# Conv stage of a mixture-of-experts block: the layer norm in two phases, with more convolution steps between a block's phases

## The chip, the cores and the metric

The kernel runs on one core of one Trainium2 chip. The core has five engines, each with its own instruction queue that is worked through in order: TensorE (PE, matrix multiply, with its weight loads shown as PEld), VectorE (DVE), ScalarE (ACT), GpSimd (POOL) and SyncE (SP), and 16 DMA engines that move data between HBM and the on-chip memory. The metric is the time on the device in microseconds (us), the median of three runs. The profile is of another execution, in which the profiler was running; that one took 6457.23 us, and its trace spans 6455.5 us.

## The reference, cut to what matters

Two layers follow each other. Layer 0 takes `x` of shape (32, 128, 56, 56) and does

```python
x = depthwise_conv7x7(input, dw_kernel) + dw_bias           # per channel
x = (x - mean_c(x)) / sqrt(var_c(x) + 1e-6) * ln_gamma + ln_beta   # over the 128 channels of a pixel
logits = x @ Wg + bg                                         # 8 experts, best 2 of each pixel
# mixture of experts with a capacity, in an order of priority
out = input + x + layer_scale * moe(x, logits)
```

Layer 1 is a 3x3 dilated convolution, a batch norm, a Gelu, an attention and a gate in Fourier space, and a residual. The change touches layer 0 alone, and there only the part up to `logits`: the depthwise convolution, the norm over channels, the multiplication by `ln_gamma`, the addition of `ln_beta`, and the product with `Wg`. Everything is in float32.

## The kernel before, in words

The kernel has three stages: the conv stage (this change), a search of each expert's threshold with the experts' matrix products, and layer 1.

**Groups and steps.** The 32 images are taken in 8 groups of 4. A group's convolution is made in `NS = 16` steps of 8 channels (`conv`, L121 to L149). A step loads two tiles, `xt` (784 KB of pixels) and `wt` (448 KB of a banded form of the taps), through SyncE's DMA queue into pools with 3 buffers each. TensorE then makes two PSUM banks `psa` of it (L136), and VectorE evicts each bank into the group's tile `y` with the bias added (L144). `y` holds 128 pixels on its partitions, 98 columns and 128 channels; it has 2 buffers. A buffer of `xt` comes free, and so the load for three steps later can start, when the matmuls of its step are done.

**Blocks and phases.** When all 16 steps of a group are done, every pixel has its 128 channels, and the norm can be made. The group's 98 columns are cut into 7 blocks (`sizes`): six of 16 columns and one of 2. `block` returns the phases of one block as closures:

- `stats`: VectorE takes `bn_stats` of each column (L161), some small operations (L165 to L171), a square root on ScalarE (L172), and a reciprocal and the bias `nb` (L173, L174);
- `norm`: ScalarE normalises each column in place, sixteen activations per block (L181); VectorE then multiplies by `gB` and adds `bB`, over the whole block (L185), and ScalarE's queue issues the store of the block to HBM (`xf<-y`, L188). ScalarE's queue stands still until VectorE is done with the block;
- `across`: TensorE transposes the block into four PSUM banks `pyt` (L196), ScalarE copies them out as `yT` (L198);
- `logits`: TensorE multiplies by `Wg` (L206), ScalarE copies the result `lq` (L215);
- `back`: TensorE transposes it again (L220), VectorE adds `bg` (L223).

After the last block, `choose` finds the two best experts of each pixel on VectorE (L263 to L302, some 17 operations of up to 1.5 us) and stores three numbers per pixel as `meta` in 64-byte rows (`xf<-meta`, L299).

**What sets the order.** `plan` makes a table from convolution step to phases: phase number `i` of block `b` stands at step `b*3//2 + i`. While group g+1 is convolved, each step is followed by the phases of group g that stand at it, and `choose` comes one step after the last phase. With five phases the last one stands at step 13 and `choose` at 14. After the last group there are no convolution steps left, and the phases follow each other (the tail of the stage). From this program a scheduler makes each engine's order when the kernel is built; it stays close to the order written, but moves single instructions ahead where it expects room. So where `across` of a block stands in TensorE's order is fixed: TensorE waits there until the block is normalised, and every convolution step behind it waits with it. As built, TensorE's order in a group is: steps 0, 1, 2, transposes of block 0, step 3, transposes of block 1, and so on, the transposes of the last block after step 11, and then steps 12 to 15 with nothing but the last logits between them.

Of the kernel before, what the change touches and what calls it, by code (L numbers as in the profile page):

```python
# [71 lines left out]
def conv_seq_kernel(ctx: ExitStack, tc: tile.TileContext, t: dict, out: bass.AP, dbg: dict):  # L72
# [41 lines left out]
    with tc.tile_pool(name="a1", bufs=1) as a1, tc.tile_pool(name="a2", bufs=2) as a2, tc.tile_pool(  # L114
# [9 lines left out]
        def conv(g, c0, y):  # L124

            xt = a3.tile([PK, CB, 4 * NCB * NB], F32, name="xt")
            nc.sync.dma_start(out=xt, in_=t["x8"][g, c0 // CB])
            wt = a3.tile([PK, CB, 2, P8 * P8], F32, name="wt")
            nc.sync.dma_start(out=wt, in_=t["wt"][c0 // CB])
            xv = xt.rearrange("k c (h n q) -> k c h n q", h=2, n=2)  # L130
            for c4 in range(0, CB, 4):
                ps = bank("psa")
                for c in range(4):
                    for b in range(2):
                        for h in range(2):
                            nc.tensor.matmul(  # L136
                                ps[h * 64 : (h + 1) * 64, c * TG : (c + 1) * TG],
                                lhsT=wt[:, c4 + c, b, :],
                                rhs=xv[:, c4 + c, h, :, b * NB : b * NB + NP],
                                start=(b == 0),  # L140
                                stop=(b == 1),
                            )
                cs = slice(c0 + c4, c0 + c4 + 4)
                nc.vector.tensor_tensor(  # L144
                    out=y[:, :, cs],
                    in0=ps[:, : 4 * TG].rearrange("p (c t) -> p t c", c=4),
                    in1=dwbB[:, cs].unsqueeze(1).broadcast_to([128, TG, 4]),
                    op=ALU.add,
                )  # L149

        def block(g, y, lg, t0, n):
# [26 lines left out]
            def norm():  # L178
                for i in range(n):
                    yi = y[:, t0 + i, :]  # L180
                    nc.scalar.activation(  # L181
                        yi, yi, AF.Identity, scale=sd[:, i : i + 1], bias=nb[:, i : i + 1]
                    )
                for w, op in ((gB, ALU.mult), (bB, ALU.add)):
                    nc.vector.tensor_tensor(  # L185
                        out=yb, in0=yb, in1=w.unsqueeze(1).broadcast_to([128, n, C]), op=op
                    )
                nc.scalar.dma_start(out=xfv[:, g * TG + t0 : g * TG + t0 + n, :C], in_=yb)  # L188
# [40 lines left out]
            else:  # L229
# [12 lines left out]
                def back():  # L242
# [4 lines left out]
                        op=ALU.add,  # L247
                    )

            return [stats, norm, across, logits, back]  # L250

        def choose(g, lg):

# [55 lines left out]


        NS = C // CB
        sizes = [16] * (TG // 16) + ([TG % 16] if TG % 16 else [])

        def plan(g, y):
            lg = a2.tile([128, TG, E], F32, name="lg")
            at = {}
            t0 = 0
            for b, n in enumerate(sizes):
                for i, phase in enumerate(block(g, y, lg, t0, n)):
                    at.setdefault(b * 3 // 2 + i, []).append(phase)  # L320
                t0 += n
            last = max(at)
            at[last + 1] = [lambda: choose(g, lg)]
            return at

        behind = {}
        for g in range(HI // 2):
            y = a2.tile([128, TG, C], F32, name="y")
            for k in range(NS):
                conv(g, k * CB, y)  # L330
                for phase in behind.pop(k, []):
                    phase()
            for k in sorted(behind):
                for phase in behind[k]:
                    phase()
            behind = plan(g, y)
# [970 lines left out]
```

## Time and profile before

| | |
|---|---|
| Time, median of 3 runs | 5591.87 us (5589.1 to 5595.34) |
| Span of the profiled execution | 6455.5 us, 85506 instructions |
| Busy: PE, PEld, DVE, ACT, POOL | 76%, 52%, 48%, 32%, 41% of the span |
| Conv stage in the trace | from the start to about 1068 us, then the store of the last `meta` to 1083.5 us |
| In the conv stage: `conv` matmuls L136 | 424.2 us busy |
| `norm` on ScalarE, L181 | 311.0 us busy, 784 activations, 488 ns each |
| `gB` and `bB` on VectorE, L185 | 48 of each for full blocks, 2284 and 2272 ns |
| transposes L196, idle time of PE ahead of them | 154.7 us busy, 304.4 us idle |

How to read it: a row of a group of instructions has the line, the engine, the operation, its operands by name and how many there were, then the busy time of the group, the mean duration of one, and behind a second bar the idle time of that engine just ahead of these instructions, with what ended it. A row of a window has the busy time of every engine in that stretch of the trace, the clock that TensorE was granted, the busy share of the DMA engines (it can go above 1 where packets overlap) and what they moved. Starts and ends of single instructions are read from the timeline.

### The profile page before, as it was taken

To read this page: it belongs to the slowest core of one execution; us is meant where nothing else is said; L and a number is where in the kernel's file an instruction comes from. 1 tells how busy PE (TensorE), PEld (TensorE's weight loads), DVE (VectorE), ACT (ScalarE), POOL (GpSimd) and SP (SyncE) were. 2 spreads that over 40 slices of the span, in tenths; PEclk is the share of its full clock that TensorE was granted. 3 is DMA by queue.
4 is the path that set the end of the run, shared out by engine and by line. 5 is a ranking of instruction groups with operands and counts; after the bars stand their busy time and mean duration, and the time that the engine had idled before them with its cause. 6 is when DMAs were issued, how large, how long until landed. Compare 5 with 4: busy or idle time off the path is not lost.

```text
span 6455.5 us, 85506 instructions
## 1 busy us (share of the span) xinstructions
PE 4925.6 (76%) x32850; PEld 3344.5 (52%) x32850; DVE 3087.3 (48%) x6927; ACT 2090.8 (32%) x3595; POOL 2616.6 (41%) x2564
## 2 busy tenths in 40 slices
PE   6666653598887989999984677777776876777678
PEld 5555552376665756766762344434444443444445
DVE  4676675565656655345221334434443443444346
ACT  2445543132232323333330223333332333333235
POOL 0000000344353435444436645565555545555450
PEclk8888885799999999999996778888887887888789
DMA  9999983122222222222233233333333333333331
GB/s 229 220 233 214 227 201 83 36 65 62 52 67 51 70 54 69 68 70 72 70 110 70 64 83 99 92 85 75 96 94 84 96 91 82 81 93 95 83 97 44
DMA packets 616216, 634.08 MB, mean 98 GB/s; under 512 B 166145, under 2 KB 540546, under 8 KB 611714
## 3 DMA queue, kind: packets, MB, share of 16 engines
q1 hardware_dynamic: 332418, 395.64, 22.2%
q0 software_dynamic: 81664, 175.18, 12.7%
q10 hardware_dynamic: 201728, 57.81, 4.6%
q8 instruction: 260, 4.26, 0.3%
q14 instruction: 146, 1.20, 0.1%
HBM read 454.98 MB, written 173.41 MB: 97 GB/s over the span
## 4 chain that ended last, share of the span: by engine, by line
PE 35%; issue 14%; another core or an unknown queue 12%; POOL 11%; DVE 6%; ACT 3%; DMA 3%; DVEq 0%; POOLq 0%; ACTq 0%; SPq 0%
PE pf L895 8%; PE py L715 7%; PE ph L705 6%; POOL xg L671 6%; PE pm L939 5%; POOL y L850 4%; PE pt L931 3%; DMA xg<-xf,ids 2%; PE pg L963 1%; PE pxt L677 1%; PE pxs L872 1%; PE pim L1030 1%; DVE junk L416 1%; ACT oa L1043 1%
## 5 line engine op out<-in xcount | busy, mean ns | idle before, releaser
L850 POOL DMA_INDIRECT y<-yf,slot x1568 | 1640.2, 1046 | 1324.5 <-DVE xs L864 816.1
L671 POOL DMA_INDIRECT xg<-xf,ids x984 | 964.9, 981 | 1393.6 <-PE pxt L677 531.0
L895 PE MATMUL pf<-xp,cw 128*64 128x448 f32 x4032 | 1029.3, 596 | 186.1 <-issue 185.4
L708 ACT ACTIVATE hT<-ph,b1t 128x512 f32<-128x512 f32 (+1 forms) x992 | 673.3, 682 | 1468.7 <-PE ph L705 1282.1
L715 PEld LDWEIGHTS py<-W,hT 128*128 128x128 f32 x7872 | 951.5, 195 | 251.5 <-ACT hT L708 124.8
L715 PE MATMUL py<-W,hT 128*128 128x128 f32 x7872 | 1000.6, 281 | 98.9 <-DVE gat L682 41.7
L705 PE MATMUL ph<-xT,W 128*128 128x512 f32 (+1 forms) x1984 | 910.0, 598 | 6.6 <-issue 6.5
L895 PEld LDWEIGHTS pf<-xp,cw 128*64 128x64 f32 x4032 | 319.1, 146 | 732.9 <-issue 704.7
L933 DVE COPY mid<-pt 112x512 f32<-112x512 f32 (+3 forms) x480 | 307.4, 661 | 707.0 <-PE pt L931 327.1
L705 PEld LDWEIGHTS ph<-xT,W 128*128 128x128 f32 x1984 | 361.1, 194 | 346.6 <-issue 341.2
L136 PE MATMUL psa<-xt,wt 112*64 112x98 f32 x8192 | 424.2, 267 | 87.0 <-DMA wt<-in_wt_dram 74.8
L136 PEld LDWEIGHTS psa<-xt,wt 112*64 112x64 f32 x8192 | 400.9, 150 | 125.3 <-issue 66.9
L682 DVE SCALAR_TENSOR_TENSOR gat<-xg 128x4 f32<-128x4 f32 (+2 forms) x256 | 42.2, 165 | 780.6 <-DMA xg<-xf,ids 779.3
L288 POOL MEMSET meta<- 128x1568 f32 x8 | 11.2, 1406 | 958.2 <-DMA xf<-meta 851.7
L196 PE MATMUL pyt<-ident,y 128*128 128x128 f32 x784 | 154.7, 378 | 304.4 <-DVE nb L174 150.7
L942 ACT COPY T<-pm 128x464 f32<-128x464 f32 (+2 forms) x240 | 123.1, 520 | 643.2 <-PE pm L939 382.6
L864 DVE TENSOR_TENSOR xs<-xs,y 128x896 f32<-128x896 f32 x224 | 243.1, 1085 | 175.0 <-DMA y<-yf,slot 80.9
L181 ACT ACTIVATE y<-y,nb,sd 128x128 f32<-128x128 f32 x784 | 311.0, 488 | 16.9 <-DVE nb L174 16.9
L196 PEld LDWEIGHTS pyt<-ident,y 128*128 128x128 f32 x784 | 138.6, 201 | 331.1 <-issue 229.3
L144 DVE TENSOR_TENSOR y<-psa,dwbB 128x392 f32<-128x392 f32 x256 | 143.6, 563 | 327.7 <-PE psa L136 327.5
L1017 ACT COPY Q<-pm 128x464 f32<-128x464 f32 (+1 forms) x128 | 63.8, 511 | 692.1 <-remote 502.2
L877 DVE TENSOR_TENSOR xp<-xp,pxs 128x256 f32<-128x256 f32 x448 | 146.4, 383 | 255.3 <-remote 147.8
(376 smaller groups left out, 6479.1 us busy)
## 6 DMA issues: line engine op xcount, KB each, us to landing
xt<-in_x_dram SPq DMA_DIRECT2D x128, 784.0 KB
yf<-yo SPq DMA_DIRECT2D x240, 256.0 KB
xp<-in_xp_dram SPq DMA_DIRECT2D x32, 1832.0 KB
wt<-in_wt_dram SPq DMA_DIRECT2D x128, 448.0 KB
xs<-xf SPq DMA_DIRECT2D x112, 448.0 KB
xf<-y ACTq DMA_DIRECT2D x48, 1024.0 KB
y<-yf,slot POOLq DMA_INDIRECT x1568
out_dram<-oa SPq DMA_DIRECT2D x224, 112.0 KB
```

The lines of the kernel that those rows point to most:

```text
L136: nc.tensor.matmul(ps[h * 64 : (h + 1) * 64, c * TG : (c + 1) * TG], lhsT=wt[:, c4 + c, b, :], rhs=xv[:, c4 + c, h, :, b * NB : b * NB + N ...
L181: nc.scalar.activation(yi, yi, AF.Identity, scale=sd[:, i : i + 1], bias=nb[:, i : i + 1])
L196: nc.tensor.transpose(pt[:, i * 128 : (i + 1) * 128], y[:, t0 + i0 + i, :], ident)
L671: nc.gpsimd.indirect_dma_start(out=xg[:n, q, :], out_offset=None, in_=xf, in_offset=bass.IndirectOffsetOnAxis(ap=ids[:n, c0 + q : c0 + q + ...
L705: nc.tensor.matmul(ph[:, :ns], lhsT=W1[:, e, f * C : (f + 1) * C], rhs=xT[:, :ns], start=True, stop=True)
L708: nc.scalar.activation(hT[:, f, :ns], ph[:, :ns], AF.Gelu, bias=b1t[:, e, f : f + 1])
L715: nc.tensor.matmul(py[:n, q * C : (q + 1) * C], lhsT=hT[:, f, q * 128 : q * 128 + n], rhs=W2[:, e, f, :], start=(f == 0), stop=(f == FF // ...
L850: nc.gpsimd.indirect_dma_start(out=y[:, m, :], out_offset=None, in_=yf, in_offset=bass.IndirectOffsetOnAxis(ap=s[:, r * NB + m : r * NB + ...
L864: nc.vector.tensor_tensor(out=xs, in0=xs, in1=y, op=ALU.add)
L895: nc.tensor.matmul(pf[i * DD : (i + 1) * DD, : 8 * W], lhsT=cw[:, k, :], rhs=xps[i][:, o : o + 8 * RP].rearrange("p (h w) -> p h w", w=RP) ...
L933: dve(mid[:m, :ni, :].rearrange("p i c -> p (i c)"), pt[:m, : ni * 128])
L939: nc.tensor.matmul(pm[:, i * M : (i + 1) * M], lhsT=mid[:m, i, :], rhs=by, start=True, stop=True)
```

## The change

`norm` is cut in two. `norm` keeps the sixteen activations of ScalarE, and the new phase `affine` has VectorE's two operations and the store. The phases of a block no longer stand at consecutive steps: the tuple `BEHIND` says how many steps behind the block's first each one stands. `affine` stands two steps after `norm`, so that `across` stands at `b*3//2 + 4` in place of `+ 2`, and the two phases after it move by two as well. With the last phase at step 15, `choose` stands at 16, after the last step. No operation is added or taken away, and no buffer. It is meant to give a block's normalisation time to finish before TensorE's queue comes to its transposes.

```diff
@@ -181,6 +181,8 @@
                     nc.scalar.activation(
                         yi, yi, AF.Identity, scale=sd[:, i : i + 1], bias=nb[:, i : i + 1]
                     )
+
+            def affine():
                 for w, op in ((gB, ALU.mult), (bB, ALU.add)):
                     nc.vector.tensor_tensor(
                         out=yb, in0=yb, in1=w.unsqueeze(1).broadcast_to([128, n, C]), op=op
@@ -247,7 +249,7 @@
-            return [stats, norm, across, logits, back]
+            return [stats, norm, affine, across, logits, back]
@@ -309,6 +311,7 @@
         NS = C // CB
+        BEHIND = 0, 1, 3, 4, 5, 6
         sizes = [16] * (TG // 16) + ([TG % 16] if TG % 16 else [])
@@ -316,7 +319,7 @@
             for b, n in enumerate(sizes):
-                for i, phase in enumerate(block(g, y, lg, t0, n)):
+                for i, phase in zip(BEHIND, block(g, y, lg, t0, n)):
                     at.setdefault(b * 3 // 2 + i, []).append(phase)
                 t0 += n
             last = max(at)
```

As built, TensorE's order in a group of the changed kernel is: steps 0 to 4, transposes of block 0, step 5, transposes of block 1, and so on, the transposes of the last block after step 13, and then steps 14 and 15. On VectorE the first part of `choose` now stands among the evictions of steps 14, 15 and of the next group's step 0, and its second part between that step 0 and the next group's first statistics. From the threshold search on, every engine's order is as it was.

## The prediction

> **What bounds the kernel now.** I read the change's stage alone, first its windows by group, then one group closely, then the tail. In the windows below (us from the start; busy time of PE, PEld, DVE, ACT, POOL; granted clock, DMA share, GB/s) the rows are a stretch of group 0, which has no phases beside it, two later groups, the last group, and the tail with the store of the last `meta`.
>
> ```profile
> 15.00:98.00 83.00, 60.84 (x1057) 58.05 (x1056) 22.38 (x51) 0.00 (x0) 0.00 (x0) 0.86 1.03 255
> ...
> 344.00:467.00 123.00, 79.25 (x1215) 68.97 (x1211) 84.48 (x224) 58.99 (x139) 1.40 (x1) 0.81 0.94 227
> 467.00:590.00 123.00, 81.23 (x1200) 71.12 (x1200) 83.47 (x223) 59.00 (x139) 1.40 (x1) 0.81 0.94 224
> ...
> 836.00:952.00 116.00, 74.29 (x1122) 64.61 (x1118) 77.81 (x212) 58.60 (x138) 1.41 (x1) 0.82 0.87 207
> 952.00:1083.70 131.70, 38.55 (x174) 26.20 (x174) 74.63 (x205) 60.21 (x140) 1.40 (x1) 0.60 0.35 77
> ```
>
> Group 0 runs at the rate of the loads, 255 GB/s. The later groups take 123 us each, no engine is busy over 84.5 us of it, and the DMA engines move 224 to 227 GB/s: near their limit, not at it. Where they fall off is seen in 6 us windows of the group that starts at 464.7 us:
>
> ```profile
> 494.70:500.70 6.00, 1.24 (x14) 0.21 (x10) 6.00 (x31) 6.00 (x17) 0.71 (x1) 0.88 0.99 266
> 500.70:506.70 6.00, 2.04 (x10) 2.07 (x11) 3.97 (x6) 4.84 (x13) 0.00 (x0) 0.50 0.24 68
> 506.70:512.70 6.00, 6.00 (x80) 5.11 (x82) 1.45 (x4) 3.83 (x10) 0.00 (x0) 0.77 0.44 123
> ```
>
> TensorE stood still and freed no buffer, so the loads ran dry. The timeline says at what:
>
> ```profile
> 476.95 6.26 ACT L181 ACTIVATE y<-y,nb,sd 128x128 f32<-128x128 f32 x16 [2.01 <-DVE nb L174]
> ...
> 488.10 3.65 PE L196 MATMUL pyt<-ident,y 128*128 128x128 f32 x16 [12.42 <-DVE nb L174]
> ...
> 491.61 2.05 ACT L198 COPY yT<-pyt 128x512 f32<-128x512 f32 x4 [7.99 <-PE pyt L196]
> ...
> 504.66 3.65 PE L196 MATMUL pyt<-ident,y 128*128 128x128 f32 x16 [8.72 <-DVE df L168]
> ```
>
> The transposes of block 0 came after a wait of 12.4 us, those of block 1 after 8.7 us; the releaser named is a VectorE operation next to the affine's last one, which ended at 487.95 and 504.51. ScalarE in turn waited 8.0 us for the transposes. So the engines run in turn, and the convolution steps queue behind.
>
> **What the Trainium skill says.** "DMA: Bandwidth & Descriptors", Issuing engines are not separate DMA queues: loads issued by SyncE and stores issued by ScalarE end on the same 16 DMA engines. The trace agrees: 255 GB/s of loads alone in group 0, 224 to 227 of both together. So moved stores give no bandwidth. "VectorE: DVE Perf Modes", The perf-mode tier table: a float32 `tensor_tensor` of 2048 elements is held to the plain mode, 2293 ns; the trace has 2284 and 2272. Cutting the phase does not make it cheaper. "Perfetto Trace Analysis", Optimization Strategy: a gap that repeats can mean too few buffers. Here it is rather the order: what ended TensorE's waits is VectorE's work on `y`.
>
> **The change part by part.** I put the changed order of instructions on each engine beside the durations of this trace and followed one group by hand, from the first eviction of its step 0 (0 us; before, 464.7).
>
> 1. *`choose` moves.* Before, its last 8 or so operations lie behind that eviction; after, some 6 more of 0.97 us and two small ones do, and they delay the first block's `nb` from 12.2 us to 20.7. Behind them on VectorE wait the statistics and the evictions of steps 1 and 2; for these TensorE has free banks.
>
> 2. *The first transposes.* Norm of block 0 is 20.8 to 27.1 (6.26), affine to 32.7 (2.27 + 2.25 and a reciprocal, behind the eviction of step 4). Before, 23.3. But TensorE has two more steps to do, and at 5 us per step (1.262 MB by 255 GB/s) steps 3 and 4 are not loaded before some 25 to 30 us. The wait of 12.4 us falls to 3 to 8 us, and three loads are in flight meanwhile.
>
> 3. *Later blocks.* Before, the store of block 0 is issued at 23.3 and that of block 5 at 89.9: 13.3 us per block. ScalarE's own part is 6.26 + 2.05 + 0.58 (`lq`) + 0.37 (issue) = 9.3 us, the rest is waiting. After, ScalarE's order has the norm of block b+1 ahead of `yT` of block b, so it normalises while VectorE and TensorE finish the block before. What still holds it is the store's issue, which waits for the affine. Followed by hand: norm 1 from 32.9 to 39.2 (its `nb` stands behind affine 0), `yT` 0 to 41, then idle until affine 1 ends at 48.2 (VectorE has the statistics of blocks 3 and 4, 3.4 us each, and step 5's evictions ahead of it); norm 2 to 55, `yT` 1 to 57, norm 3 to 63.4, `lq`, store 2 at 64, `yT` 2 to 66.4; store 3 waits for affine 3, 63.4 + 4.7 = 68.1; norm 4 to 74.8, `yT` 3 to 77.7, norm 5 to 84, store 4 at 85, `yT` 4 to 89, store 5 at 89.5. That is 11.4 us per block. Block 6 has two columns; its transposes come after steps 12 and 13 and `yT` 5 (97 us), at 105.5; before, at 102.5. So the chain of blocks starts 9.4 us later and ends 3 us later.
>
> 4. *The steps behind it.* Before, steps 12 to 15 and the next step 0 follow the last transposes: 567.6 to 587.6 us, 20 us, 4 us a step, partly waiting for loads. After, 14, 15 and 0 follow: some 10.5 us. The two steps that moved to the front of the group lie under the wait for block 0. Sum: 105.5 + 10.5 = 116 us for a group; before, (832.2 - 95.9)/6 = 122.7.
>
> 5. *Can the DMA engines do that?* Loads of 16 x 1.262 MB at 254 GB/s are 79.5 us, stores of `y`, 6.4 MB at 290 GB/s (the best slices of the tail), 22 us. The `meta` store took 16.2 us alone; beside loads it costs between 0 and 16, so the limit lies between 102 and 118 us. I take the middle, 110: the chain of 116 sets the group. As only three loads can be ahead, some of the waits for loads will not fit, and I add 1 us: 117 us for a group, between 113 (no waits for loads at all) and 122 (as tight as now).
>
> 6. *The tail.* No step lies in it. Before, blocks' stores are issued from 976.3 to 1042.8 us, 13.3 us each, and the last logits are added at 1053.25. By hand, after: `nb` of block 0 comes 6 us later (the rest of `choose`), but the norms of blocks 0 and 1 run back to back, and stores come 983.8, 990, 1007, 1011, 1027, 1032: 9.6 us per block. The last logits are added at 1041, 12 us earlier. `choose` (14 us) and the store of `meta` (16.2 us) follow unchanged. I give 5 to 14 us.
>
> Cutting the phase itself costs nothing, since the instructions are the same. No new wait for a buffer comes of it: `y`'s buffer is rewritten by step 0 two groups on, at 116, 10 us after its last read at 106.
>
> Sum in the trace: seven groups with phases x 5.7 + 12 = 52 us. The timed runs are 5591.87 / 6455.5 = 0.866 of the trace, and which part of the trace the profiler stretches isn't known; I take the same for this stage: 45 us, 5547.
>
> **The rivals.**
> *A, the transfers bind anyway.* The DMA share of 0.94 in the windows of whole groups speaks for it, the windows of 0.24 and 0.44 against it. Groups stay at 122.7 and the tail alone gains: 12 x 0.866 = 10 us, 5582.
> *B, slower.* The wait is moved, not removed: block 0 starts 9 us later, ScalarE is held by the store's issue, and the last block's store now lies close to the step that rewrites `y`, a wait that could take the place of the old one. If a group gets 4 us longer and the tail gains nothing: 7 x 4 x 0.866 = 24 us, 5616. Against it: TensorE still has slack at both ends of the group.
> *C, more than I take.* The 20 us behind the last transposes were mostly waits for loads, and `meta` costs nothing beside loads: 113 us per group and 14 in the tail, (7 x 9.7 + 14) x 0.866 = 71 us, 5521.
>
> **How the numbers follow.** My forecast 0.62, C 0.18, A 0.12, B 0.08. The predicted time is the forecast's, 5547. From C's 5521, with its bounds, the range goes down to 5512; up it takes in A and the forecast with a tail of 5 us, 5588; B and the outer part of A and C are left out, under 2 in 10. The bound for faster is 5580.7: the forecast, C and a little of A, 0.82; within 0.2% most of A and the edge of B, 0.10; slower 0.08.
>
> **What would show it.** In the changed profile: groups of 115 to 118 us; the wait ahead of a group's first transposes at 8 us or less; `yT`'s wait for transposes well under 24.4 us per group; no 6 us window of a middle group under 0.6 of DMA share; the last store of a group at about 100 us; the last logits some 12 us sooner after the last eviction than before (101 us there). Wrong I would be if TensorE's waits appear unshortened at block 1 or later, if an eviction of step 0 waits for stores, or if the stage's time in timed runs is set by faster transfers than under the profiler.

## The result, and the profile after

The changed kernel took 5513.84 us (median of four runs, 5502.47 to 5518.05) against 5591.55 us: a ratio of 0.9857 with a 95% interval of 0.984 to 0.9874. It is faster, by 78 us where 45 were forecast, and lies at the lower end of the range (5512 to 5588). The direction holds, and so does the part of the mechanism that is the later place of the transposes; the split of the norm gives nothing to the time, and the sizes do not hold.

The trace of before that the prediction used (6455.5 us) was of an execution with an unusually slow layer 1 (3087 us from its first load to the end). A second trace of the same kernel, *before_again*, spans 5599.3 us, as the timed runs do, with 2270 us of layer 1, and its conv stage is like the first one's, 1082.6 against 1083.7 us. All comparisons below are with this second trace. From the end of the conv stage on the two kernels are alike: 4516.7 us before, 4521.4 after. The stage itself went from 1082.6 to 992.4 us.

The windows of the second trace of before, groups 1 to 3 (columns as in the prediction; the last two are the DMA share and GB/s):

```profile
95.50:219.00 123.50, 82.89 (x1182) 72.58 (x1179) 77.24 (x203) 58.33 (x138) 0.00 (x0) 0.80 0.84 218
219.00:343.00 124.00, 82.26 (x1199) 72.29 (x1198) 83.44 (x221) 58.94 (x139) 1.40 (x1) 0.80 0.95 224
343.00:466.00 123.00, 82.54 (x1214) 72.34 (x1212) 82.98 (x221) 58.98 (x139) 1.41 (x1) 0.80 0.92 222
```

The same of the changed kernel: group 0, groups 1, 2 and 4, the last group, and the tail.

```profile
15.00:93.00 78.00, 57.22 (x1052) 54.33 (x1048) 20.33 (x45) 0.00 (x0) 0.00 (x0) 0.89 1.03 263
93.00:190.00 97.00, 76.40 (x1171) 63.73 (x1173) 70.68 (x192) 56.88 (x137) 0.00 (x0) 0.91 1.02 272
190.00:306.40 116.40, 81.55 (x1203) 69.30 (x1200) 83.08 (x221) 58.49 (x139) 1.40 (x1) 0.83 1.02 239
...
422.00:535.70 113.70, 80.35 (x1204) 67.53 (x1202) 83.19 (x221) 58.65 (x139) 1.40 (x1) 0.86 1.00 241
...
762.60:875.40 112.80, 79.08 (x1166) 66.24 (x1162) 82.48 (x221) 58.64 (x139) 1.40 (x1) 0.85 0.94 223
875.40:992.40 117.00, 37.31 (x174) 22.90 (x174) 78.85 (x211) 58.91 (x140) 1.41 (x1) 0.64 0.39 87
```

Two things are to be seen. Group 1 fell from 123.5 to 97 us and moves 272 GB/s; the groups behind it fell only to between 112.8 and 116.4. And the DMA share, 0.92 to 0.96 in the middle groups before, is now 1.00 to 1.03. It counts the time that packets took, overlapping or not, so a share of 1 doesn't say that no more could be moved. The granted clock in these rows is somewhat higher after, but TensorE's busy time is nearly the same (82.3 us in group 2 before, 81.6 after): what went is idle time. (Groups run from the first eviction of their step 0 to that of the next; group 1 is the first with phases beside it, and no `choose` and no `meta` store of an earlier group lies in it.)

One group followed by the timeline, group 4, in us from its first eviction:

| | before | after |
|---|---|---|
| TensorE's wait ahead of the first transposes | 12.6 | 9.5 |
| sum of its waits ahead of all transposes | 35.0 | 10.2 |
| stores of blocks issued, first and last | 23.3, 98.1 | 29.4, 96.2 |
| last transposes end | 103.2 | 104.1 |
| from there to the next group | 18.7 | 9.6 |
| length of the group | 121.9 | 113.7 |

The chain of blocks ends where it ended before. What shrank is the stretch behind it. The waits ahead of the transposes fell by 24.8 us, but the group by only 8.2: a part of the waiting moved to the phases behind. TensorE's waits of group 4 after, from 422 to 535.7 us (us in total, times, longest):

```profile
PE pyt L198 <- DVE nb L174: 10.2, 2, 9.5
PE plq L208 <- ACT yT L200: 9.1, 2, 7.3
PE pl L222 <- ACT lq L217: 7.9, 2, 5.1
PE psa L136 <- DMA wt<-in_wt_dram: 6.2, 5, 2.1
```

Before, it waited 35.0 us ahead of `across` and 7.6 ahead of the convolution's matmuls, and not at all ahead of `logits` and `back`. Now 17.0 us stand ahead of these two, for ScalarE's copies `yT` and `lq`; the sum fell from 42.6 to 33.4 us. (Behind `affine` the lines of the changed kernel's file stand two further down: L196 is L198, L188 is L190.)

ScalarE's waits, first before, then after, both from 400 to 520 us:

```profile
ACT yT L198 <- PE pyt L196: 24.6, 16, 8.0
...
ACT y L181 <- DVE nb L174: 2.0, 1, 2.0
```

```profile
ACT y L181 <- issue: 11.3, 1, 11.3
...
ACT yT L200 <- PE pyt L198: 7.9, 9, 3.0
ACT y L181 <- DVE nb L174: 5.1, 3, 2.6
```

The wait of `yT` for transposes fell from 24.6 to 7.9 us. A new one has come: 11.3 us before one norm, ended by nothing that an engine did ("issue"). ScalarE's timeline of the changed kernel shows what stood ahead of it:

```profile
440.44 6.26 ACT L181 ACTIVATE y<-y,nb,sd 128x128 f32<-128x128 f32 x16 [2.59 <-DVE nb L174]
...
451.42 6.72 ACTq L190 DMA_DIRECT2D xf<-y  x1
458.19 6.26 ACT L181 ACTIVATE y<-y,nb,sd 128x128 f32<-128x128 f32 x16 [11.29 <-issue]
```

The median of the store issues takes 0.37 us; this one held ScalarE's queue for 6.72 us, while the `meta` store of the group before was being moved. In groups 2 to 7 this first store's issue takes 4.9 to 7.6 us. `meta` is not needed for it, though: in group 1, which has none ahead of it, the second block's store is held for 4.80 us. The 6 us windows of that time in group 4 show it from the side of the DMA engines:

```profile
446.00:452.00 6.00, 0.51 (x3) 0.54 (x4) 5.98 (x12) 0.90 (x3) 0.00 (x0) 0.50 1.09 273
452.00:458.00 6.00, 5.86 (x79) 5.46 (x77) 6.00 (x33) 0.00 (x0) 0.00 (x0) 0.77 1.74 87
458.00:464.00 6.00, 0.00 (x0) 0.00 (x0) 3.00 (x17) 5.81 (x16) 1.40 (x1) 0.80 0.98 240
464.00:470.00 6.00, 4.11 (x15) 1.50 (x16) 5.52 (x11) 3.96 (x12) 0.00 (x0) 0.63 0.56 149
```

In the first row TensorE stands at the first transposes, and yet 273 GB/s are moved; the row at the first transposes before (484.3 to 490.3 us) had 163 GB/s. Before, the loads ran dry at the second block's transposes (a share of 0.24 in the prediction's window); after, there is still a row of 0.56. In the second row the share is 1.74 but only 87 GB/s are moved: these are for the most part the 64-byte rows of `meta`. The view of the DMA queues from 430 to 460 us counts them (packets, MB, share of 16 engines; the first queue has the loads, the second ScalarE's stores):

```profile
q1 hardware_dynamic: 1162, 5.56, 67.1%
q10 hardware_dynamic: 13199, 1.13, 51.4%
```

1.13 MB in 13199 packets took 51.4% of 30 us, 15.4 us, where 5.56 MB of loads took 20.1 us. 12560 of these packets are `meta`'s, 0.80 MB and 14.2 us; the rest are the beginning of the first block's store.

The `meta` store holds something else as well. Before, every load was issued as soon as the matmuls that free its buffer were done. A row of TensorE's timeline, one of SyncE's, and a line of SyncE's waits, all of group 4 after:

```profile
454.94 2.92 PE L136 MATMUL psa<-xt,wt 112*64 112x98 f32 x64
...
460.45 0.31 SPq L127 DMA_DIRECT2D xt<-in_x_dram  x1
...
SPq L127 <- DMA xf<-meta: 17.6, 1, 17.6
```

The load is that of step 8. Its buffer was free when step 5's matmuls ended at 457.9 us, but it was issued at 460.45, after the last packets of `meta` (459.2). The same load comes 2.4 to 3.6 us late in five of the groups 2 to 7; what ties it to `meta`'s landing the traces don't say.

### The profile page after: what moved, and what is told of

It reads as the page before. It is cut to its first block, busy times and chain, and to the rows that moved or that the text cites. A ratio compares the mean times of both kernels' runs of the same rounds, so it can differ in the third digit from the quotient of the medians.

```text
span 5513.8 us, 85629 instructions
## 1 busy us (share of the span) xinstructions
PE 4653.0 (84%) x32850; PEld 3226.8 (59%) x32850; DVE 3073.9 (56%) x6927; ACT 2097.5 (38%) x3595; POOL 2613.8 (47%) x2564
## 4 chain that ended last, share of the span: by engine, by line
POOL 28%; PE 25%; issue 19%; DVE 7%; DMA 6%; ACT 2%; ACTq 0%; POOLq 0%; DVEq 0%; SPq 0%
POOL y L853 17%; POOL xg L674 10%; PE py L718 6%; PE ph L708 5%; PE pf L898 4%; PE pm L942 4%; DMA xg<-xf,ids 3%; DMA y<-yf,slot 2%; PE pt L934 2%; PE pg L966 1%; ACT y L181 1%; PE psa L136 1%; PE pxt L680 1%; DVE junk L419 1%; DVE y L187 1%
## 5 line engine op out<-in xcount | busy, mean ns | idle before, releaser
L898 PE MATMUL pf<-xp,cw 128*64 128x448 f32 x4032 | 885.9, 566 | 0.9 <-DVE xp L880 0.8
L898 PEld LDWEIGHTS pf<-xp,cw 128*64 128x64 f32 x4032 | 289.0, 141 | 465.9 <-issue 439.7
L136 PE MATMUL psa<-xt,wt 112*64 112x98 f32 x8192 | 413.1, 262 | 83.2 <-DMA wt<-in_wt_dram 74.9
L136 PEld LDWEIGHTS psa<-xt,wt 112*64 112x64 f32 x8192 | 389.4, 146 | 121.4 <-issue 67.0
L731 DVE TENSOR_TENSOR yo<-py,b2t 128x512 f32<-128x512 f32 (+2 forms) x256 | 169.8, 666 | 112.1 <-PE py L718 111.3
L198 PE MATMUL pyt<-ident,y 128*128 128x128 f32 x784 | 137.8, 347 | 92.0 <-DVE nb L174 57.9
L680 PE MATMUL pxt<-ident,xg 128*128 128x128 f32 (+1 forms) x984 | 195.2, 280 | 11.0 <-DMA xg<-xf,ids 10.8
L1033 PE MATMUL pim<-feat,meanw 128*128 128x448 f32 x224 | 126.4, 651 | 92.2 <-ACT gt L1088 92.2
```

The costliest lines, as they stand in the source:

```text
L136: nc.tensor.matmul(ps[h * 64 : (h + 1) * 64, c * TG : (c + 1) * TG], lhsT=wt[:, c4 + c, b, :], rhs=xv[:, c4 + c, h, :, b * NB : b * NB + N ...
L680: nc.tensor.transpose(pt[:, q * 128 : q * 128 + n], xg[:n, q, :C], ident[:n, :n])
L898: nc.tensor.matmul(pf[i * DD : (i + 1) * DD, : 8 * W], lhsT=cw[:, k, :], rhs=xps[i][:, o : o + 8 * RP].rearrange("p (h w) -> p h w", w=RP) ...
```

## The experiments

The theories, as the expectations number them: 1, the later place of the transposes in TensorE's order makes the gain; 2, the split of norm and affine makes it; 3, `choose`'s later place matters by itself; 4, the `meta` store's hold of ScalarE's queue is what keeps the groups behind group 1 at 114 us; 5, it is `choose`, which stands ahead of the first block (in *meta_pool* its time on VectorE, in *no_choose* together with its store); 6, it is the transfers (in *no_choose* those of loads and `y` stores, or the chain of blocks itself). The ratio is to the kernel before on the same chip.

| kernel | us | ratio, 95% interval | group 1 | groups 2 to 6, DMA share | last eviction to last logits |
|---|---|---|---|---|---|
| before_again | 5601.29, one run | | 123.5 | 122.7, 0.94 | 101.4 |
| changed | 5513.84 | 0.9857, 0.984 to 0.9874 | 97.2 | 114.5, 1.02 | 86.8 |
| after_again | 5509.61 | 0.9839, 0.9825 to 0.9852 | 99.2 | 114.0, 1.01 | 87.0 |
| unsplit_far | 5510.8 | 0.9843, 0.9827 to 0.986 | 104.7 | 112.5, 1.00 | 87.7 |
| split_near | 5551.98 | 0.9915, 0.9898 to 0.9931 | 109.6 | 119.4, 0.98 | 89.5 |
| choose_16 | 5598.41 | 1.0, 0.9991 to 1.0009 | 121.1 | 122.8, 0.94 | 101.4 |
| unsplit_farther | 5555.82 | 0.9932, 0.9916 to 0.9949 | 106.7 | 116.6, 0.98 | 95.2 |
| choose_next | 5508.17 | 0.9848, 0.9831 to 0.9864 | 98.9 | 113.1, 1.02 | 85.7 |
| unsplit_next | 5573.41 | 0.9956, 0.994 to 0.9973 | 106.0 | 124.2, 0.92 | 89.0 |
| meta_pool | 5504.18 | 0.9829, 0.9809 to 0.9849 | 97.7 | 110.1, 0.97 | 89.2 |
| meta_pool_again | 5502.56 | 0.9826, 0.9813 to 0.9839 | 97.3 | 109.4, 0.96 | 90.1 |
| unsplit_pool | 5505.76 | 0.9824, 0.981 to 0.9837 | 104.2 | 111.9, 0.94 | 87.9 |
| no_choose | not compared | | 106.7 | 102.4, 1.00 | 77.8 |

**The kernel before, once more** (*before_again*), for a second trace:

> The kernel before, unchanged, for a second trace. The first trace of it spans 6455 us where timed runs take 5592; the traced run of the changed kernel took no longer than its timed ones. If the profiler stretches this kernel, the span is near 6455 again and its conv stage (start to the end of the last meta store) is near 1083 us; if the first trace was an odd run that was slow in layer 1, the span is near 5592, and the groups of the conv stage take about 122 us as in the first trace.

It is the trace used above.

**The transposes later, without the split** (*unsplit_far*, on the kernel before): norm and affine stay one phase, and the transposes get their new place.

```diff
+        BEHIND = 0, 1, 4, 5, 6
...
-                for i, phase in enumerate(block(g, y, lg, t0, n)):
+                for i, phase in zip(BEHIND, block(g, y, lg, t0, n)):
```

> norm and affine stay one phase, and only the transposes and what follows them move two steps back (offsets 0, 1, 4, 5, 6). Theory 1, the place of the transposes in TensorE's order makes the gain: groups 2 to 7 near 115 us and 5510 to 5530 us. Theory 2, splitting the norm makes it, as VectorE's affine and the store's issue come later than the next block's norm: groups near 120 us and over 5570 us.

All of the gain is there: 0.9843. So the later place makes it, and the split adds nothing to the time. It does something, though: group 1 takes 104.7 us without it and 97.2 with it. In the later groups that advantage is gone, 112.5 against 114.5. The windows of groups 1 and 4 without the split:

```profile
98.00:201.00 103.00, 78.78 (x1172) 65.29 (x1170) 69.73 (x191) 56.69 (x137) 0.00 (x0) 0.88 0.96 254
...
428.00:541.00 113.00, 84.43 (x1211) 71.75 (x1209) 82.96 (x222) 58.29 (x139) 1.41 (x1) 0.83 0.99 245
```

**The split, without the later place** (*split_near*): the six phases at consecutive steps, so that the transposes come one step later than before, not two.

```diff
-        BEHIND = 0, 1, 3, 4, 5, 6
+        BEHIND = 0, 1, 2, 3, 4, 5
```

> The norm split, but all phases at consecutive steps (offsets 0 to 5): transposes one step later than in the kernel before, choose at step 15. Theory 1: half the gain, groups near 118 us, 5545 to 5565 us. Theory 2: nearly the whole gain, 5510 to 5530 us. Theory 3, the later choose makes it: about half as well.

Half of the gain, as theories 1 and 3 both expected: groups of 119.4 us, 3.3 of the 8.2 us that two steps buy, and 45 of 78 us in the sum. Which of the two theories it is, the next run decides.

**`choose` later, alone** (*choose_16*, on the kernel before):

```diff
-            at[last + 1] = [lambda: choose(g, lg)]
+            at[last + 3] = [lambda: choose(g, lg)]
```

> The kernel before with choose at step 16 in place of 14, and nothing else. Theory 1: choose delays the first block's statistics by about 9 us and gives nothing back, so groups 2 to 7 are 3 to 9 us longer, 5610 to 5650 us; group 1, which has no choose ahead, stays at 122. Theory 3, the gain comes from choose (and the meta store) no longer lying among the last steps' evictions: 5510 to 5550 us.

No difference, a ratio of 1.0 within 0.001. The gain that theory 3 expected did not come, nor the loss that theory 1 expected. With the transposes at their old place, TensorE waited 13.4 us at the first block of group 4 instead of 12.6, and groups 2 to 6 took 122.8 us as before.

**The transposes later still** (*unsplit_farther*, on *unsplit_far*):

```diff
-        BEHIND = 0, 1, 4, 5, 6
+        BEHIND = 0, 1, 5, 6, 7
```

> One phase for norm and affine and the transposes three steps back (offsets 0, 1, 5, 6, 7), choose at step 17. Theory 1, each step that moves from the end of the group to its beginning gains until the wait ahead of the first transposes is gone; in the changed kernel 9.5 us of it were left, in which two more steps would fit: groups near 110 us, 5480 to 5500 us. Rival: the last blocks' phases now run past step 15, and the next group's first steps come late for it: groups at 114 us or over, 5510 to 5540 us.

The expectation of theory 1 failed, and the rival's forecast of the groups is nearer (116.6 us), though the time is longer than it said. In group 4 the last transposes end at 111.8 us in place of 103.9; 4.9 us follow them instead of 8.8, so 4 of the 8 us come back. The wait did not go, it moved one phase on: TensorE waits 6.5 us ahead of the first transposes, and then 18.3 us ahead of the first product with `Wg`, for copies `yT` that ScalarE makes only after the norms of the next blocks and a store.

```profile
494.38 3.09 PE L206 MATMUL plq<-yT,wg 128*32 128x512 f32 x8 [18.32 <-ACT yT L198]
```

ScalarE had stood for 15.8 us, to 480.9, until `meta` had landed, but in group 1, which has no `meta` ahead, TensorE waits 17.0 us at this place too. Of the distances tried, two steps more than before is the best; three is worse than that by 45 us.

**`choose` in the middle of the next group** (*choose_next* on the changed kernel, *unsplit_next* on *unsplit_far*), so that nothing of it stands ahead of the first block:

```diff
-            at[last + 1] = [lambda: choose(g, lg)]
-            return at
+            return at, lambda: choose(g, lg)
...
-        behind = {}
+        behind, late = {}, None
...
-            behind = plan(g, y)
+            held = late
+            behind, late = plan(g, y)
+            if held:
+                behind.setdefault(9, []).append(held)
...
+        late()
```

> The changed kernel with choose of a group put off by one group, to step 9 of the next but one group's steps, so neither choose nor the meta store lies ahead of the first blocks; in the tail one more choose. Theories 4 and 5: groups 3 to 7 at 98 to 106 us, and the tail some 8 us longer: 5430 to 5470 us. Theory 6: the bytes are only moved, groups stay at 112 to 115 us, 5510 to 5530 us.

> The same put-off choose on the kernel with one phase for norm and affine and the transposes two steps back (offsets 0, 1, 4, 5, 6). If the split has no part in the gain, it takes what choose_next takes, within 10 us. If ScalarE's norm ahead of the affine's wait matters once choose is gone (group 1: 97.3 us with the split, 104.7 without), it is slower by 5 x 7 = 35 us.

The gain that theories 4 and 5 expected did not come; the groups, 113.1 us, and nearly the time are where theory 6 had them. Group 4 of *choose_next* starts well, with stores at 21.0 and 35.0 us instead of 29.4 and 47.2, but the later blocks are delayed, and the last transposes end at 105.8. The longest delay there is again an issue behind `meta`: block 5's store holds ScalarE's queue for 13.1 us. Without the split it is far worse: the last transposes end at 117.3 us, and the group takes 126.6. Here the split is worth 65 us, more than the 35 of the second forecast. In the trace of *unsplit_next* ScalarE stands at a store for 5.6 us while VectorE has operations of `choose` ahead of that block's affine, and at block 5's for 12.4 us, with the copies of block 4's `yT` behind it, before which it idles for 16.8 us; with the split these copies are made ahead of that store. How much each of the two costs, no run shows.

**The `meta` store issued by GpSimd** (*meta_pool*, *meta_pool_again* on the changed kernel, *unsplit_pool* on *unsplit_far*):

```diff
-            nc.scalar.dma_start(out=xfv[:, cut, C:], in_=meta)
+            nc.gpsimd.dma_start(out=xfv[:, cut, C:], in_=meta)
```

> The changed kernel with the store of meta issued by GpSimd, which has nothing else to do in this stage, in place of ScalarE; choose stays at step 16. In the changed kernel group 1, which has no choose and no meta store ahead of it, takes 97 us and the later ones 113 to 116, and ScalarE's first store of a group sits 7 us in its queue behind the meta store. Theory 4, this hold of ScalarE is the larger part of the 17 us: groups 2 to 7 at 102 to 108 us, 5440 to 5470 us. Theory 5, choose's 10 us on VectorE ahead of the first statistics are: groups 110 to 114 us, 5490 to 5515 us. Theory 6, the DMA engines are full and the meta store's bytes cost the same from any queue: groups at 114 us, no change to 5514 us.

> The changed kernel with the meta store issued by GpSimd, once more: its conv stage was 21 us shorter in the trace, but its time only 10 us less. If the stage's gain reaches the end: 5490 to 5497 us. If half of it is lost behind the stage (layer 0's rest takes 11 us longer in its trace): 5501 to 5508 us.

> Norm and affine in one phase, the transposes two steps later as in the changed kernel, and the meta store issued by GpSimd. If the meta store's hold of ScalarE's queue costs without the split as it does with it, 4 us per group: groups of 108 to 110 us, 5495 to 5505 us. If the split is what makes use of the freed queue: groups of 111 to 113, 5508 to 5514 us.

> The changed kernel once more, beside the two with the meta store by GpSimd on the same chip: 5508 to 5518 us, groups 2 to 7 of 113 to 116 us.

The repeat of the changed kernel came as expected. With the store on GpSimd's queue the groups fall by 4 to 5 us, to 110.1 and 109.4. Theory 4's 102 to 108 is missed; groups and time are as theory 5 had them, and of the second trace's two forecasts the later one, a part lost behind the stage, came. Without the split the groups take 111.9 us against 112.5, so the move gives almost nothing there, as the second branch of that expectation said, while the time of 5505.76 lies between its two branches. ScalarE is no longer held: in groups 2 to 7 of both traces of *meta_pool* no store issue takes over 0.45 us. The loads that had come late are issued at once again, and TensorE's waits ahead of `logits` and `back` fall to some 7 to 8 us a group. The DMA time falls as well. The queues over the conv stage, first of the changed kernel (0 to 993 us), then of *meta_pool* (0 to 972 us):

```profile
q10 hardware_dynamic: 201728, 57.81, 30.2%
```

```profile
q10 hardware_dynamic: 101248, 51.38, 20.5%
q0 software_dynamic: 1792, 6.42, 3.9%
```

The eight stores leave ScalarE's queue with 100480 packets, 12560 each, and appear on GpSimd's with 1792, 224 each. Their time is 30.2% of 993 us less 20.5% of 972, some 101 us, on the one queue, and 3.9% of 972, 38 us, on the other; beside loads, in the first six of them, 12.8 to 14.4 us a store became 3.1 to 3.7. Three things change here together, ScalarE's hold, the late load and the transfer's time, and which of them gives the 4 to 5 us is open. These are the kernels with the lowest medians here, but beside the changed kernel on the same chip, 5502.56 and 5505.76 against 5509.61, the intervals overlap: a gain over it is likely, not settled. The conv stage of the two traces of *meta_pool* is 19 to 25 us shorter than in the two of the changed kernel, while the times differ by 7 to 10; behind the stage they take 4534.4 and 4526.8 us against 4521.4 and 4523.2. Why is open.

**`choose` and the `meta` store left out** (*no_choose*):

```diff
-            at[last + 1] = [lambda: choose(g, lg)]
+            if g == HI // 2 - 1:
+                at[last + 1] = [lambda: choose(g, lg)]
...
+            nc.gpsimd.dma_start(out=xfv[:, g * TG : (g + 1) * TG, C:], in_=zero)
```

> The changed kernel with choose and the meta store left out for groups 0 to 6: their meta rows are written as zeros at the start and their keys are zero, so the experts chosen for these groups, and the stages behind, are not the reference's; only the conv stage's groups are read. Theory 5 (what keeps groups 2 to 7 at 114 us where group 1 takes 97 is choose: 14 us of VectorE ahead of the first block, and its meta store): groups 2 to 7 take 95 to 100 us each, like group 1. Theory 6 (it is the transfers of loads and y stores, or the blocks' chain itself): they stay at 108 to 114 us.

The part that is left out of the listing fills keys and rows with zeros. The whole time, 6366.11 us, says nothing, since the experts get other pixels. The windows of groups 2 to 5; group 1 still has the last of the zeros' stores in it.

```profile
218.00:323.00 105.00, 80.52 (x1198) 67.95 (x1195) 69.40 (x200) 55.81 (x136) 0.00 (x0) 0.87 0.98 254
323.00:426.00 103.00, 80.89 (x1197) 67.99 (x1195) 69.56 (x200) 55.73 (x136) 0.00 (x0) 0.88 1.00 260
426.00:528.00 102.00, 80.68 (x1209) 66.66 (x1207) 69.47 (x200) 55.28 (x136) 0.00 (x0) 0.90 1.01 264
528.00:625.00 97.00, 78.65 (x1200) 65.69 (x1198) 69.41 (x200) 55.50 (x136) 0.00 (x0) 0.89 1.01 273
```

97 to 105 us, 102.4 on the mean of groups 2 to 6, with a share of 1.00: somewhat over what theory 5 expected, and clear of theory 6's 108 to 114. The wait ahead of the first transposes of group 4 is 0.7 us. So `choose` with its store makes 12 of the 17 us that separate group 1 from the rest. How much of it is VectorE's time, how much the store's transfer and how much what the store holds up, this run doesn't separate.

**Share times length.** The DMA share times the length of a group is the engine time of its packets. In groups 2 to 6 it is 115.3 us before (122.7 x 0.94), 116.8 changed, 112.5 in *unsplit_far*, 115.4 in *choose_next*, about 106 with the store issued by GpSimd, and 102.4 without it. It goes with the `meta` store and hardly with the order of the engines. Before, a group was 7 us longer than this product; after the change it is not, and no order that was tried with the store on ScalarE's queue got below 112.5 us. This fits a limit by the transfers at about 114 us, but does not show it: packets overlap, up to a share of 1.74, and in group 4 TensorE still idles for 33.4 us and a load is issued late.

## Why the prediction was too small

**Step 1**, `choose`'s move delays the first block: right in direction. The first store is issued at 29.4 us (33 forecast). The move alone costs nothing in the kernel before (*choose_16*), but *no_choose* shows the first wait of group 4 at 0.7 us where nothing of `choose` stands ahead.

**Step 2**, the wait ahead of the first transposes of 3 to 8 us: measured 9.5 in group 4 and 7.0 to 9.5 in groups 2 to 7, somewhat missed. The transfers go on meanwhile as forecast, at 273 GB/s.

**Step 3**, the chain of blocks: the last transposes forecast at 105.5, measured 104.1, and the last store at 96.2 for about 100. The new hold of ScalarE's queue behind `meta`, 6.7 us, was not foreseen, nor TensorE's new waits ahead of `logits` and `back`, 17.0 us, nor the late load; the later blocks made it up.

**Step 4**, 20 us behind the chain become 10.5: measured 18.7 and 9.6. This is the mechanism, and *unsplit_far* and *split_near* bear it out: what counts is how many steps the transposes stand back, up to two. But the prediction traced the gain to both, the split and the place (in step 3 ScalarE gains by having the next norm ahead); the split gives nothing to this kernel's time.

**Step 5**, the limit of the transfers: 102 to 118 us, with 110 taken. Without `meta` the groups took 102.4 us and group 1 97.2, at a share of 1.00 and 1.02, so 79.5 + 22 = 101.5 for loads and `y` stores was about right. What the `meta` store costs a group, put between 0 and 16.2 us, is not measured by itself: it is 12 us together with `choose`, and 4 to 5 us come back when GpSimd issues it. Its packets took 14.2 us of the engines' time. The Trainium skill, "DMA: Bandwidth & Descriptors", Specifications, gives 512 bytes as the least transfer at full rate, which the prediction did not use for this store; the trace agrees, 87 GB/s in the window of its 64-byte rows. The prediction's "So moved stores give no bandwidth" holds for `y`'s stores as far as the runs go, but not for this one: on GpSimd's queue the same bytes took a quarter of the time beside loads. Rival A's claim, that transfers bind at 122.7 us, is refuted; at 114 us it is open.

**The sum** is where it failed: "seven groups with phases x 5.7 + 12 = 52 us", times 0.866. The step that failed is the first term, one size of gain for all seven groups, and within it group 1.

- *Group 1* was taken like the others. It has no `choose` and no `meta` of an earlier group, and gained 26.3 us (123.5 to 97.2), 20.6 more than its term. This is the largest error. The chain of 116 us that was worked out for "a group" has `choose` and `meta` in it, and *no_choose* shows that leaving them out brings the other groups from 114.5 to 102.4 us. The window of before hinted at it: a DMA share of 0.84 in 123.5 us.
- *Groups 2 to 7* went from 121.9 to 114.2 us on the mean: 7.6 each in place of 5.7, 11.6 us more. The 117 us had 1 us added for waits for loads, and a chain 1.4 us too late.
- *The tail* gave 14.6 us in place of 12.
- *The factor 0.866* was wrong. The profiler did not stretch the conv stage; the trace of before was long in layer 1. That is 7 us of the 52.

Together 52 + 20.6 + 11.6 + 2.6 is some 87 us, against 90.2 of the stage in the traces, of which 3 are group 0, which has no phases and ended 3 us sooner; the timed runs differ by 78. Rival C came nearest, by group (113) and tail (14), and with its own sum unscaled, 82 us, it would have been some 4 us off. That is in part luck: its 9.7 us a group was far too little for group 1 and 2 us too much for each of the other six, and its premise that `meta` costs nothing beside loads is not borne out.

Of the signs named beforehand: groups of 115 to 118 us were 112.8 to 116.4, and group 1 97; the first wait, 9.5 us, broke its bound of 8; `yT`'s wait was 7.9 us, well under 24.4; 6 us windows of middle groups at 0.56 and, at the lowest, 0.47 of DMA share broke the bound of 0.6; the last store was issued at 96.2 us, for about 100; the last logits came 14.6 us sooner, for 12.

## What to carry to other kernels

A waiting instruction in an in-order queue costs what is queued behind it: look for the place where its input is ready by then, and try one place nearer and one farther, since both can be worse. Count the engine's waits at all its instructions, since a wait that is gone in one place can come back in the next. Before summing over repeats, look at the first and the last one by themselves; what is absent in them (here an earlier group's `choose` and store) may be the limit of all others. Before a factor is taken from timed runs to a trace, see in which stage the trace is longer.

## What the runs showed of the hardware

A store of 784 KB in 64-byte rows, issued by ScalarE, went out in 12560 packets, which took the 16 DMA engines 14.2 us in group 4 beside loads. While it was being moved, the next issue on the same queue took 4.9 to 7.6 us in groups 2 to 7, and ScalarE's arithmetic behind it waited, where the median issue took 0.37 us. An issue can be held without it: 4.80 us in group 1, up to 3.9 us in *no_choose*. A load on SyncE's queue, too, was issued only when this store had landed, 2.6 us late in group 4.

Issued by GpSimd the same store went out in 224 packets: 192 of 4096 bytes, which is 64 rows each, 16 of 1024 and 16 of 4. Beside loads they took the engines 3.1 to 3.7 us. The Trainium skill, "DMA: Bandwidth & Descriptors", SWDGE vs HWDGE vs iDMA, describes packets of preferably up to 4096 bytes for GpSimd's path, which agrees. Loads and stores together moved 272 GB/s in group 1, more than the loads alone in group 0 (263).
